# Opening loads of a fused attention and mixture-of-experts kernel: order and queues

## The chip, the cores and the metric

The kernel runs on one core of one Trainium2 chip. The metric is the device time of one execution in microseconds (us); lower is better. The engines are named as the profile names them: PE (TensorE, matrix products; PEld is its weight load), DVE (VectorE), ACT (ScalarE), POOL (GpSimd) and SP (SyncE). SP and ACT can both issue DMAs, each on a queue of its own.

## The reference

The input x has 4 x 1024 tokens of width 256, all in 32-bit floats. Two sandwiches are applied, each adding a normalized result to its input:

```
x = x + layernorm(attention_block(layernorm(x)))
x = x + layernorm(moe(layernorm(x)))
```

The attention block normalizes its input h with a gain and a bias, projects it to q, k, v (256 x 256 each), and does linear attention with 4 heads of 64: q goes through a softmax over the head's 64 channels, k through a softmax over the 1024 tokens, context = k^T v per head, output = q context. A projection wo with a bias bo and a residual follow, then a gelu layer of width 1024 (w_ff1, w_ff2) and a last projection w_d. The second part is a mixture of 8 experts with low-rank updates, of which each token uses its top 2.

## The kernel before, in words

The 4096 tokens are cut into 8 blocks of 512 (BLK), each held as a tile of 128 partitions x 4 tokens x 256; partition p holds tokens 4p to 4p+3 of the block, so a block's rows are contiguous in a partition. The attention part runs block by block through `prelude`, `front` and `middle`; the experts follow on tokens sorted by their pair of experts.

The order of work on PE, DVE, ACT and POOL is fixed when the program is built: the code is written as streams (generators), and a planner with a cost for each step picks the next stream by estimated times (`plan`, `V`, `A`, `G`, and a table `ARRIVE` of assumed arrival times of the first loads). Within an engine instructions run in this order. The first matmuls, the warm-ups of L1886 and L1887 (128 x 128 ones by ones, WARM of them), are issued without adding to the planner's clock. DMAs run in the order in which the program issues them on their queue; the order of the opening ones is written out by hand in L196 to L222.

What the opening consists of, by name and line:

- `load_z(i)` (L170) loads block i's residual x into a tile z. For blocks 0 and 1 it issues two halves, tokens 0 and 1 of each partition on SP's queue and tokens 2 and 3 on ACT's (L180, L181). Later blocks are one DMA on SP's queue.
- `load_w(eng, ...)` (L183) makes a weight tile and loads it on the queue of the engine given.
- `vec` (L197): ten kilobytes of gains and biases. `gate_s` (L201): the router's weights, 8 KB.
- `wq_raw` (L200): the raw query weights, 256 KB, columns 0 to 255 of a 512-column array. `wk_s`, `wv_s`, `wo_s` (256 KB each) and `bo_s` (128 KB as a broadcast) follow on ACT's queue, `wff2_s` (1 MB), `wd_s`, `bd_s`, blocks 2 and 3, `wff1_s` and the experts' weights on SP's.
- `prelude(i)` (L670): on DVE, mean and variance of each of the block's four token columns (`stats`, L340 and L341, a BATCH_NORM_STATS2 and an aggregate each), then `rsqrt2` (L386 on DVE, a power on POOL at L389, result `rr`), then `less_mean` (L395, `lm`) and `normalize` (L404 on DVE, L410 on ACT, alternating for block 0), which writes z in place.
- `prepare_q` (L450): scales the gate by the norm's weights (L454), forms the query bias on PE from wq_raw (`pbq`, L459), scales wq_raw into `wq_s` (first half on ACT, L462; second on DVE, L464), centres the gate (`pcg`, L441, L467), copies it beside wq_s (L469) and the bias into `bq_s` (L473), and scales `wk_s` in place on ACT (L476, L478).
- `front(i)` (L699): transposes z on PE (`pt_h`, L328) and copies it to `hT` on ACT (L719), multiplies by wq_s (`pq`, L734; L315 is the helper that issues matmuls), adds the bias on DVE (L735), then the softmax of q, the keys (`pk`, L769) and so on.

In program order on DVE, block 0's statistics and `r2a` come first, then the two gate scalings, then wq_s (L464), then lm. On ACT, wq_s (L462) comes ahead of block 0's normalization.

Of the kernel before, what the change touches and what calls it, by code (L numbers as in the profile page):

```python
# [15 lines left out]
P = 128  # L16
D = 256
DC = D // P
# [3 lines left out]
E, R = 8, 16  # L22
# [4 lines left out]
TB = 4  # L27
HT = TB // 2
# [12 lines left out]
HALF = P // 2  # L41
CLASSES = ((0, 2), (0, 3), (1, 2), (1, 3), (0, 1), (2, 3))
SHARE = 80
WARM = 14

CODE = (0.0, 1.0, 3.0, 7.0)
KINDS = [CODE[a] + CODE[b] for a, b in (*CLASSES, (0, 0), (2, 2), (1, 1), (3, 3))]
# [19 lines left out]
def sandwich_kernel(  # L67
# [23 lines left out]
    nc = tc.nc  # L91
# [67 lines left out]
    for c in range(DC):  # L159
        t = wp.tile([P, P], F32, tag=f"cbd{c}", name=f"cbd{c}")  # L160
# [4 lines left out]
    xts, zs = {}, {}  # L165

    def tokens(ap, i):
        return ap[i * BLK : (i + 1) * BLK, :].rearrange("(p t) d -> p t d", t=TB)

    def load_z(i):  # L170
        if i in (2, 3):
            zs[i] = sp.tile([P, TB, RW], F32, tag="row", name=f"z_{i}")[:, :, 0:D]
        elif i == NBLK - 1:
            zs[i] = mp2.tile([P, TB, D], F32, tag="u0", name=f"z_{i}")
        else:
            zs[i] = zp.tile([P, TB, D], F32, tag="z", name=f"z_{i}")
        if i > 1:
            nc.sync.dma_start(out=zs[i], in_=tokens(x, i))
            return
        for t, eng in ((0, nc.sync), (HT, nc.scalar)):  # L180
            eng.dma_start(out=zs[i][:, t : t + HT, :], in_=tokens(x, i)[:, t : t + HT, :])  # L181

    def load_w(eng, src, shape, name, pattern=None, **kw):  # L183
        t = wp.tile(shape, F32, tag=name, name=name)
        eng.dma_start(out=t, in_=src.rearrange(pattern, **kw) if pattern else src)
        return t

    def load_ranks(src, name):
# [5 lines left out]
        return t  # L194

    load_z(0)  # L196
    vec = load_w(nc.sync, vecs, [P, 20], "vec")  # L197
    wqv_c = wqv.rearrange("(c p) f -> p c f", p=P)
    wq_raw = mp2.tile([P, DC, D], F32, tag="m1", name="wq_raw")
    nc.sync.dma_start(out=wq_raw, in_=wqv_c[:, :, 0:D])  # L200
    gate_s = load_w(nc.scalar, gate, [P, DC, E], "gate_s", "(c p) f -> p c f", p=P)  # L201
    wk_s = load_w(nc.scalar, wk, [P, DC, D], "wk_s", "(c p) f -> p c f", p=P)
    load_z(1)
    wv_s = wp.tile([P, DC, D], F32, tag="wv_s", name="wv_s")
    nc.scalar.dma_start(out=wv_s, in_=wqv_c[:, :, D : 2 * D])
    wo_s = load_w(nc.scalar, wo, [P, DC, D], "wo_s", "(c p) f -> p c f", p=P)
    bo_s = load_w(nc.scalar, bo.partition_broadcast(P), [P, D], "bo_s")
    wff2_s = mp1.tile([P, FC, D], F32, tag="actA", name="wff2_s")
    nc.sync.dma_start(out=wff2_s, in_=wff2.rearrange("(c p) f -> p c f", p=P))
    wd_s = wp.tile([P, DC, DX], F32, tag="wd_s", name="wd_s")  # L210
# [1 line left out]
    bd_s = wp.tile([P, DX], F32, tag="bd_s", name="bd_s")  # L212
    nc.sync.dma_start(out=bd_s[:, 0:D], in_=bd.partition_broadcast(P))
    load_z(2)
    load_z(3)
    wff1_s = load_w(nc.sync, wff1, [P, DC, FF], "wff1_s", "(c p) f -> p c f", p=P)
# [75 lines left out]
    def psum(name):  # L292
        last[0] = slots.index(min(slots))
        slots[last[0]] = 1e9
        pool, tag = homes[last[0]]
        return pool.tile([P, BLK], F32, tag=tag, name=name)
# [1587 lines left out]
    with tc.manual_schedule(engines={EN.PE, EN.DVE, EN.Activation, EN.Pool}):  # L1884
        warm = psum("warm")
        for _ in range(WARM):  # L1886
            nc.tensor.matmul(warm[:, 0:P], lhsT=ones, rhs=ones, start=True, stop=True)  # L1887
# [154 lines left out]
```

## Time and profile before

| | us |
|---|---|
| median of 3 runs (979.72 to 980.01) | 980.0 |
| profiled execution | 980.27 |
| span of the profiled execution, first to last instruction | 978.2 |
| PE busy | 960.9 |
| first warm-up matmul starts, last one ends | 1.13, 6.12 |
| first matmul on loaded data (pbq) | 8.38 |
| first query projection (pq) | 10.99 |
| last matmul ends | 968.6 |

The mean granted clock of TensorE is 0.998 of full speed. [...] An idle engine costs time only if the work that ends last hangs on it. DMA rows on SPq and ACTq show the issuing alone; the data land later, which is seen in the rows that wait for them.

The opening issues, from the timeline (start on its queue in us): on SP block 0's first half 0.74, vec 1.18, wq_raw 1.65, block 1's first half 2.12, wff2 4.14, wd 8.85, bd 9.28, block 2 9.80, block 3 behind it, wff1 11.68, w1 14.69; on ACT block 0's second half 0.74, gate 1.18, wk 1.66, block 1's second half 2.18, wv 4.32, wo 4.73, bo 5.25 (until 6.16).

### The profile page before, as it was taken

The page shows a single profiled execution, that of the slowest core. Times are in us where ns is not written, and L with a number is a line of the kernel's source. Part 1 is how long each engine was busy: PE and PEld are TensorE (multiplying, and loading weights), DVE is VectorE, ACT ScalarE, POOL GpSimd, SP SyncE. Part 2 cuts the span into 40 slices and gives each one's busy share as a digit, 9 for nine tenths or more (in the row PEclk, how much of TensorE's full clock was granted, in tenths as well). Part 3 has the DMA queues.
Part 4 walks back from the last instruction along what each step waited for, and adds up shares of the span by engine and source line. Part 5 has one row for each costly group of instructions (what it writes and reads, how often), then busy time and mean ns, then how long its engine had stood idle before and what let it go on. Part 6 is the DMA issues. An engine that isn't in the chain of part 4 may idle for free. (4 is left out here: it accounts for less than half of the span.)

```text
span 978.2 us, 12098 instructions
## 1 busy us (share of the span) xinstructions
PE 960.9 (98%) x4235; PEld 644.5 (66%) x4235; DVE 466.6 (48%) x1423; ACT 337.9 (35%) x703; POOL 423.2 (43%) x472
## 2 busy tenths in 40 slices
PE   8999999999999999999999999999999999999996
PEld 7778888888888888887664463644636446364444
DVE  7777666656655465556413323333233332323134
ACT  5545644245223113221214425254252542522110
POOL 2101202201321221324745938759387593885442
PEclk9999999999999999999999999999999999999999
DMA  9604610100120111321100201102011020110000
GB/s 298 183 22 130 144 55 12 67 0 17 61 77 12 45 55 23 116 71 40 45 22 1 70 23 44 44 5 69 20 44 43 1 65 3 44 33 22 0 1 24
DMA packets 33745, 50.14 MB, mean 51 GB/s; under 512 B 5296, under 2 KB 24848, under 8 KB 33680
## 3 DMA queue, kind: packets, MB, share of 16 engines
q1 hardware_dynamic: 29088, 39.36, 14.3%
q0 software_dynamic: 3072, 8.51, 2.4%
q10 hardware_dynamic: 1520, 1.45, 0.4%
q8 instruction: 35, 0.57, 0.2%
q14 instruction: 30, 0.25, 0.1%
HBM read 28.18 MB, written 17.19 MB: 46 GB/s over the span
## 5 line engine op out<-in xcount | busy, mean ns | idle before, releaser
L315 PE MATMUL ph<-tT,w_s 128*128 128x512 f32 (+1 forms) x576 | 235.6, 554 | 0.2
L315 PEld LDWEIGHTS ph<-tT,w_s 128*128 128x128 f32 x576 | 105.4, 190 | 122.1 <-issue 110.5
L315 PE MATMUL py<-wff2d,g 128*128 128x264 f32 x512 | 119.2, 386 | 0.0
L315 PEld LDWEIGHTS py<-wff2d,g 128*128 128x128 f32 x512 | 97.3, 190 | 16.6
L1435 DVE TENSOR_TENSOR act<-act,ph 128x512 f32<-128x512 f32 (+1 forms) x96 | 55.8, 594 | 96.5 <-PE ph L315 51.8
L1485 POOL TENSOR_TENSOR actA<-act,act 128x512 f32<-128x512 f32 x32 | 40.6, 1270 | 133.7 <-DVE act L1435 125.5
L1797 ACT COPY py<-ph 128x512 f32<-128x512 f32 x94 | 53.2, 571 | 120.6 <-PE ph L315 119.8
L1426 ACT ACTIVATE act<-ph 128x512 f32<-128x512 f32 (+1 forms) x96 | 48.6, 521 | 117.0 <-PE ph L315 92.5
L315 PE MATMUL pf<-h2T,wff_s 128*128 128x256 f32 x384 | 87.0, 380 | 0.0
L1435 DVE TENSOR_TENSOR act<-act,py 128x512 f32<-128x512 f32 x48 | 32.9, 685 | 103.7 <-ACT act L1426 103.7
L315 PEld LDWEIGHTS pf<-h2T,wff_s 128*128 128x128 f32 x384 | 72.1, 190 | 10.8 <-issue 1.3
L1021 ACT ACTIVATE g<-pf,bff 128x256 f32<-128x256 f32 x128 | 52.1, 475 | 75.5 <-PE pf L315 74.5
L315 PE MATMUL po<-w_s,actA 128*128 128x256 f32 x256 | 60.5, 383 | 0.0
L1245 POOL DMA_INDIRECT rows<-x,to x32 | 33.5, 1047 | 61.8 <-DVE x L1148 18.5
L315 PE MATMUL po<-w_s,actB 128*128 128x256 f32 x256 | 59.3, 379 | 0.0
L315 PEld LDWEIGHTS po<-w_s,actB 128*128 128x128 f32 x256 | 48.6, 190 | 12.2 <-issue 6.2
L315 PEld LDWEIGHTS po<-w_s,actA 128*128 128x128 f32 x256 | 46.9, 190 | 12.4 <-issue 7.0
L315 PE MATMUL ph<-u,bw 32*128 32x512 f32 x192 | 54.4, 640 | 0.0
L315 PE MATMUL py<-u,bw 32*128 32x512 f32 x192 | 54.4, 640 | 0.0
L356 POOL TENSOR_TENSOR rs_x<-rsa_x,neghalf 128x4 f32<-128x4 f32 x15 | 16.1, 1075 | 77.9 <-DVE rsa_x L352 46.1
L1048 DVE TENSOR_TENSOR y<-py,bd_s 128x264 f32<-128x264 f32 x32 | 13.8, 432 | 74.0 <-PE py L315 73.8
L1485 POOL TENSOR_TENSOR actB<-act,act 128x512 f32<-128x512 f32 x31 | 39.7, 1279 | 19.9 <-DVE act L1435 19.9
(300 smaller groups left out, 1605.6 us busy)
## 6 DMA issues: line engine op xcount, KB each, us to landing
rows<-none SPq DMA_DIRECT2D x4, 1052.0 KB
kept<-x SPq DMA_DIRECT2D x8, 526.0 KB
x<-in_x_dram SPq DMA_DIRECT2D x8, 512.0 KB
row<-rows SPq DMA_DIRECT2D x7, 526.0 KB
z<-in_x_dram SPq DMA_DIRECT2D x6, 512.0 KB
w_s<-in_w_dram SPq DMA_DIRECT2D x3, 1024.0 KB
bw<-b_s SPq DMA_DIRECT2D x24, 128.0 KB
wff_s<-in_wff_dram SPq DMA_DIRECT2D x2, 1024.0 KB
```

The costliest lines, as they stand in the source:

```text
L315: nc.tensor.matmul(out_, lhsT=lhsT, rhs=rhs, start=start, stop=stop, **kw)
L356: nc.gpsimd.tensor_tensor(r, a, neghalf[:, 0:n], ALU.pow)
L1021: nc.scalar.activation(g[:, k * W : (k + 1) * W], pf[:, k * W : (k + 1) * W], AF.Gelu_apprx_tanh, bias=bff1_s[:, f : f + 1],)
L1048: nc.vector.tensor_tensor(y[:, j % HT, :], py[:, 0:DX], bd_s, ALU.add)
L1245: ins = nc.gpsimd.indirect_dma_start(out=dst[:, :], out_offset=bass.IndirectOffsetOnAxis(ap=at, axis=0), in_=src, in_offset=None, bounds_c ...
L1426: nc.scalar.activation(to, h, AF.Silu)
L1435: nc.vector.tensor_tensor(to, to, h3, ALU.mult)
L1485: lambda x0=x0, x1=x1, op=op: nc.gpsimd.tensor_tensor(ac, x0, x1, op))
L1797: nc.scalar.copy(py[a], ph[a])
```

## The change

Block 0 is loaded in four quarters, one token column of every partition each, columns 0 and 2 on SP's queue, 1 and 3 on ACT's. Block 1 becomes one DMA on SP's queue. vec and gate move behind the quarters on ACT's queue; wq_raw comes behind the quarters on SP's; block 1, wk, wv, wo and bo follow it on SP's. Three of the fourteen warm-ups go. The whole diff:

```
-WARM = 14
+WARM = 11
...
-        if i > 1:
+        if i:
             nc.sync.dma_start(out=zs[i], in_=tokens(x, i))
             return
-        for t, eng in ((0, nc.sync), (HT, nc.scalar)):
-            eng.dma_start(out=zs[i][:, t : t + HT, :], in_=tokens(x, i)[:, t : t + HT, :])
+        for t in range(TB):
+            eng = nc.scalar if t % 2 else nc.sync
+            eng.dma_start(out=zs[i][:, t, :], in_=tokens(x, i)[:, t, :])
...
     load_z(0)
-    vec = load_w(nc.sync, vecs, [P, 20], "vec")
+    vec = load_w(nc.scalar, vecs, [P, 20], "vec")
+    gate_s = load_w(nc.scalar, gate, [P, DC, E], "gate_s", "(c p) f -> p c f", p=P)
     wqv_c = wqv.rearrange("(c p) f -> p c f", p=P)
     wq_raw = mp2.tile([P, DC, D], F32, tag="m1", name="wq_raw")
     nc.sync.dma_start(out=wq_raw, in_=wqv_c[:, :, 0:D])
-    gate_s = load_w(nc.scalar, gate, [P, DC, E], "gate_s", "(c p) f -> p c f", p=P)
-    wk_s = load_w(nc.scalar, wk, [P, DC, D], "wk_s", "(c p) f -> p c f", p=P)
     load_z(1)
+    wk_s = load_w(nc.sync, wk, [P, DC, D], "wk_s", "(c p) f -> p c f", p=P)
     wv_s = wp.tile([P, DC, D], F32, tag="wv_s", name="wv_s")
-    nc.scalar.dma_start(out=wv_s, in_=wqv_c[:, :, D : 2 * D])
-    wo_s = load_w(nc.scalar, wo, [P, DC, D], "wo_s", "(c p) f -> p c f", p=P)
-    bo_s = load_w(nc.scalar, bo.partition_broadcast(P), [P, D], "bo_s")
+    nc.sync.dma_start(out=wv_s, in_=wqv_c[:, :, D : 2 * D])
+    wo_s = load_w(nc.sync, wo, [P, DC, D], "wo_s", "(c p) f -> p c f", p=P)
+    bo_s = load_w(nc.sync, bo.partition_broadcast(P), [P, D], "bo_s")
```

The planner's costs and its `ARRIVE` table are not touched.

## The prediction

> **What bounds the kernel now.** I read the page first, then the busy time by stretches, and with these the waits and the timeline of the first 20 us. The page and the stretches (columns: from:to, length, then busy time and instructions of PE, PE's weight load, DVE, ACT, POOL, then clock, DMA share, GB/s):
>
> ```profile
> PE 960.9 (98%) x4235; PEld 644.5 (66%) x4235; DVE 466.6 (48%) x1423; ACT 337.9 (35%) x703; POOL 423.2 (43%) x472
> ```
>
> ```profile
> 1.13:4.25 3.12, 3.12 (x14) 3.12 (x15) 0.10 (x1) 0.00 (x0) 2.95 (x59) 1.00 0.71 208
> 4.25:6.12 1.87, 1.87 (x16) 1.69 (x14) 1.77 (x7) 0.00 (x0) 0.15 (x2) 1.00 0.84 272
> 6.12:8.38 2.26, 0.01 (x2) 0.03 (x1) 0.81 (x6) 1.40 (x2) 1.05 (x1) 1.00 0.97 308
> 8.38:10.99 2.61, 2.37 (x17) 2.03 (x17) 2.05 (x12) 2.08 (x5) 0.00 (x0) 1.00 1.08 367
> 10.99:20.00 9.01, 9.01 (x42) 6.40 (x43) 8.60 (x26) 5.99 (x12) 2.50 (x6) 1.00 1.08 372
> 20.00:60.00 40.00, 39.88 (x217) 31.41 (x216) 27.32 (x74) 23.39 (x51) 3.46 (x5) 1.00 0.52 153
> ```
>
> From 10.99 us, when the first query projection (pq) starts, TensorE hardly stops: it idles 0.12 us from 20 to 60, 0.54 from 60 to 440, 2.05 from 440 to 480 and 1.34 from 480 to its last matmul at 968.6. So this change can move the end only by moving that 10.99 us, and whatever it moves there should arrive almost whole at the end. The opening, by the timeline (start, length, engine, line, operation; in brackets the idle time before and what ended it):
>
> ```profile
> 4.15 0.43 DVE L340 BATCH_NORM_STATS2 st_in<-z 128x6 f32<-128x256 f32 x1 [4.15 <-DMA z<-in_x_dram]
> ...
> 6.41 0.17 DVE L386 TENSOR_SCALAR r2a_x<-mv_in 128x4 f32<-128x4 f32 x1
> ...
> 6.67 1.05 POOL L389 TENSOR_TENSOR rr_x<-r2a_x,neghalf 128x4 f32<-128x4 f32 x1 [2.26 <-DVE r2a_x L386]
> 8.27 0.35 DVE L464 TENSOR_SCALAR wq_s<-wq_raw,vec 128x256 f32<-128x256 f32 x1 [1.38 <-DMA wq_raw<-in_wqv_dram]
> ...
> 8.53 0.15 DVE L395 SCALAR_TENSOR_TENSOR lm_z<-mv_in,rr_x 128x4 f32<-128x4 f32 x1
> ...
> 8.72 1.09 ACT L410 ACTIVATE z<-z,lm_z,rr_x 128x256 f32<-128x256 f32 x2
> ...
> 10.35 1.07 ACT L719 COPY hT<-pt_h 128x512 f32<-128x512 f32 x2 [0.53 <-PE pt_h L328]
> ```
>
> Two arrivals set it. Block 0's first half is visible at 4.15; four pairs of statistics, 0.53 us each, lead to r2a at 6.41 and the root on POOL from 6.67 to 7.72. The second is wq_raw: DVE would need it after its gate work, about 6.89, but it comes at 8.27, and the small lm (8.53), which every normalization needs, is queued behind it on DVE although the root was ready at 7.72. From lm the chain runs through the normalized quarters (the last on ACT until 9.81), transposes, the hT copy at 10.35 and pq at 10.99: 2.46 us.
>
> The rate at which data arrives, in forty slices of 0.25 us from 0 to 10 us:
>
> ```profile
> GB/s 0 0 0 0 0 0 0 139 229 377 344 377 377 245 174 131 197 229 246 291 275 254 291 287 303 344 381 311 340 279 262 274 295 299 365 377 393 381 381 373
> ```
>
> Adding slices (rate times 0.25 us): 131 KB have moved at 2.35, 262 KB at 2.72, block 0's 524 KB at 3.50. DVE sees its half at 4.15, so 0.65 us lie between the last bytes in the mean and the release.
>
> **The change, part by part.**
>
> *Block 0 in quarters on two queues (L180).* Two issues become four, two on each queue, 0.39 to 0.47 us each by the rows, so at 0.74 and about 1.18. Statistics of the first quarter can start when it has landed, provided a reader waits only for its own part of the tile. That parts are tracked is seen in the trace: pq's first matmul starts at 10.99 while the two hT copies, 10.35 to 11.42, still run. If SP's quarter arrived alone it would be visible at 2.35+0.65=3.0; if the two queues share evenly, at 2.72+0.65=3.37. An upper bound is today's 4.15. I take 3.3, near the even share, since both queues issue at 0.74. The fourth quarter is needed only at 3.3+3x0.53=4.9 and all of block 0 was in by about 4.15. Then r2a is at 3.3+2.26=5.56, the root starts 0.26 later as today and ends at 5.82+1.05=6.87, lm starts at 6.95 (0.08 from a root to its next user, as POOL's 14.35 to 14.43). Against 8.53: 1.58 us.
>
> *wq_raw right behind it (L200), without vec before it and wk and half of block 1 beside it.* Ahead of its last byte are 524+262 KB, and vec and gate (18 KB) beside it: 804 KB, which today have moved at 4.88, hence visible at 5.5. That estimate was too good before: wq_raw, wk and all ahead of them were 1,066 KB, moved at 5.83, so it should have been visible at 6.5 and came at 8.27, 1.8 later. Bounds 5.5 and 7.3. I take 6, nearer the first, since now only 18 KB ride on the other queue. What does it have to meet? DVE's scaling (0.35) must end by lm at 6.95, ACT's (0.51) by 7.1, and on PE pbq and pcg (1.30 from 8.38 to 9.68) must not delay the last quarter's transpose: all three say about 6.6. So 6 costs nothing; each us past 6.6 costs one.
>
> *vec and gate on ACT's queue.* Third and fourth issues there, about 1.6 to 2.5; needed at r2a+0.09=5.65. Everything issued up to 2.6 and moved by 4.25 (648 KB) is visible near 4.9. Nothing to pay. ACT's queue is then done at 2.5 instead of 6.16, and its table load (6.19 to 7.47) moves ahead; it had 0.79 us to spare and would otherwise bind at 7.47.
>
> *Block 1 whole, and wk, wv, wo, bo on SP.* ACT's queue falls from seven issues to four (two quarters, vec, gate); SP loses vec and has one more piece of block 0 and wk, wv, wo, bo ahead of wff2. SP's waits show what an issue waits for:
>
> ```profile
> SPq L211 <- DMA wk_s<-in_wk_dram: 4.3, 1, 4.3
> ...
> SPq L209 <- DMA z<-in_x_dram: 1.5, 1, 1.5
> ```
>
> wff2, the ninth load or so in order, waited for the first half of block 0, wd for wk: eight are in flight. Now the first eight are four quarters, vec, gate, wq, block 1; wk waits for the first quarter (3.3), then one issue per 0.45 us follows. Block 1 is wanted by DVE at 10.76-1.65=9.1; 804+524=1,328 KB had moved at 6.63, visible 7.3, or 9.1 with the same 1.8 us of lateness. wk is wanted by ACT at 11.31-1.65=9.7 and by pk at 13; 1,590 KB, 7.45+0.65=8.1. wff2 is wanted at 18, block 2 at 17.4; the bytes ahead of them are those of today and the queue starts sooner. The later issues of SP (b1, w3, b3, w2, b2 until 37.5, then x, block 4) go out no later, and the first use of x is L376 at 63.9. If the cover of 1.8 us for block 1 is gone, DVE, 8.6 of 9.0 us busy there, is late by the difference.
>
> *Three fewer warm-ups (L1886).* They add nothing to the planner's clock, so the order of all else stays. Fourteen are 28 records: 14 in the 3.12 us to 4.25 (223 ns each), 14 in the next 1.87 (134 ns). Six fewer at 134 ns end at 5.32 instead of 6.12. PE then waits for wq anyway: nothing, unless the array is slow at pbq. The trace bounds that: the step is 1.07 us ahead of 5.32, and 2.26 us of idling at 6.12 did not undo it (pbq at 379 ns like later ones).
>
> [...]
>
> **The sum.** lm 1.58 earlier. The transposes gain 0.07 more: the last quarter is ready at 9.81 today, but PE, still behind pbq and pcg, transposes it at about 9.68+3x0.13=10.07, 0.26 later, of which a handover (0.05) and a weight load (0.14) remain when PE is free. So pq starts 1.65 us earlier, at 9.34. The profiled execution took 980.27 (span 978.2, 2.1 around it): 978.6. The median, 980.0, is 0.27 below it; against it, 978.4.
>
> **Rivals.**
> 1. *wq_raw still comes last*, at 7.3 by the lateness of before. For it: DVE, ACT and PE all waited for it. Against: its company on the other queue is gone. Gain 8.27-7.3=1.0: 979.0.
> 2. *More than forecast*: the first quarter alone at 3.0 or before, and block 1 or the weights so early that some of the 4 us of later PE idling go too. 1.95 or more: 977.9. Against: both queues issue at once.
> 3. *Absorbed or not split*: DVE waits for the whole tile at 4.15, so lm waits for today's root (7.72, then 7.8): gain 0.7; or DVE, 95% busy up to 20 us, gives it back. 979.3 to 980. Against: the tracked parts above; the same DVE work starts earlier too.
> 4. *Slower*: PE cools. wq_raw is no earlier than today, PE idles from 5.32 for over 3.1 us (as long as it took to speed up) and pbq, the transposes and pq run slow for 3.12 us: 14 records at 89 ns more, 1.25 us, and the wait beyond 8.27 itself, 0.15 us. 981.4. It decides from wq_raw at 8.4 on; past 9.0 it is over 0.2%.
>
> **How the numbers follow.** Forecast 0.57 (978.1 to 978.8), rival 1 0.16, rival 2 0.14, rival 3 0.08, rival 4 0.05. The range 977.7 to 979.4 holds the forecast, most of rivals 1 and 2, 0.82 in all. 0.2%, about what a measurement of this kernel can tell from no change, is 1.96 us, just above the forecast's gain: faster by more 0.20 (rival 2 and the forecast's best end), slower by more 0.04, within 0.76.
>
> **What would show it.** First statistics at 3.3, their four in 0.53 us steps without a wait, r2a at 5.6, root at 5.8, lm at 7.0, pq at 9.3, warm-ups ending at 5.3, no DVE wait for wq_raw that holds lm, no wait for block 1, wk or wff2; PE idle after pq still 4 us. Wrong if statistics start after 3.6, if lm follows wq_raw rather than the root, or if PE shows new gaps between 10 and 60 us.

## The result, and the profile after

| | before | after |
|---|---|---|
| median (range), runs | 979.53 (979.26 to 981.25), 22 | 981.23 (979.74 to 984.86), 22 |
| profiled execution, its span | 980.27, 978.2 | 979.83, 977.8 |
| first statistics (DVE) | 4.15 | 3.86 |
| gate seen by DVE | not waited for | 7.59 |
| wq_raw seen | 8.27 (DVE) | 5.64 (ACT) |
| lm | 8.53 | 8.13 |
| first query projection pq | 10.99 | 10.47 |

The ratio of after to before is 1.0018, with a 95% interval of 1.0011 to 1.0024: the change costs 0.18%, where the forecast was a gain. The profiled execution of after is one of its shortest, and that of before one of its longer ones. A reader who compares only these two sees a gain of 0.44 us.

The page of after, its busy line:

```profile
PE 962.1 (98%) x4229; PEld 644.8 (66%) x4229; DVE 466.8 (48%) x1423; ACT 338.1 (35%) x703; POOL 423.7 (43%) x472
```

PE has six records fewer and is busy 1.2 us longer. The busy time by stretches says where (from:to, length, busy time and instructions of PE, its weight load, DVE, ACT, POOL, then clock, DMA share, GB/s):

```profile
1.13:6.20 5.07, 5.06 (x22) 4.77 (x22) 2.17 (x9) 0.56 (x1) 3.12 (x60) 1.00 0.78 253
6.20:8.76 2.56, 2.06 (x9) 1.54 (x9) 1.25 (x7) 1.67 (x3) 1.05 (x1) 1.00 0.99 331
```

All 22 records of the eleven warm-ups take 230 ns each, so they end at 6.20 and not at the forecast 5.3, and pbq still runs partly slow (1.50 us instead of 1.10). In before the step to 134 ns came after 14 of 28 records. The timeline of after in the opening:

```profile
3.86 0.43 DVE L341 BATCH_NORM_STATS2 st_in<-z 128x6 f32<-128x256 f32 x1 [3.86 <-DMA z<-in_x_dram]
...
5.64 1.28 ACT L463 ACT_TABLE_LOAD   x1 [5.64 <-DMA wq_raw<-in_wqv_dram]
...
6.12 0.17 DVE L387 TENSOR_SCALAR r2a_x<-mv_in 128x4 f32<-128x4 f32 x1
6.37 1.05 POOL L390 TENSOR_TENSOR rr_x<-r2a_x,neghalf 128x4 f32<-128x4 f32 x1 [1.96 <-DVE r2a_x L387]
...
7.59 0.36 DVE L455 TENSOR_SCALAR gate_s<-gate_s,vec 128x8 f32<-128x8 f32 x2 [1.31 <-DMA gate_s<-in_gate_dram]
...
8.13 0.15 DVE L396 SCALAR_TENSOR_TENSOR lm_z<-mv_in,rr_x 128x4 f32<-128x4 f32 x1
...
10.47 0.49 PE L316 MATMUL pq<-wq_s,hT 128*128 128x264 f32 x1 [0.24 <-ACT hT L720]
```

Three things are to be seen. wq_raw comes early, as forecast. The root is ready at 7.42, but lm stands behind the gate's scaling on DVE, and the gate, 8 KB, is seen only at 7.59. And ACT's table load has not moved ahead: it now stands behind the arrival of wq_raw (5.64), where in before it stood behind nothing but ACT's own issues (from 6.19, the last issue ending at 6.16). The rate at which data arrives, in slices of 0.25 us from 0:

```profile
GB/s 1 0 0 0 0 0 0 33 184 180 242 311 381 353 238 270 324 306 287 306 346 314 412 352 329 378 345 329 336 356 365 377 352 258 246 209 213 168 168 156
```

Added up, 262 KB have moved at 3.07 us, against 2.72 in before's profile. The rows of block 0 are 1 KB long now instead of 2 KB, but that this is the reason is not shown: the four profiles with the loads of before reach 262 KB anywhere from 2.72 to 3.03 us (b_w11 the latest), those with quarters from 2.79 to 3.07.

### The profile page after: what moved, and what is told of

It reads as the page before. It is cut to its first block, busy times and chain, and to the rows that moved or that the text cites. A ratio compares the mean times of both kernels' runs of the same rounds, so it can differ in the third digit from the quotient of the medians.

```text
span 977.8 us, 12085 instructions
## 1 busy us (share of the span) xinstructions
PE 962.1 (98%) x4229; PEld 644.8 (66%) x4229; DVE 466.8 (48%) x1423; ACT 338.1 (35%) x703; POOL 423.7 (43%) x472
```

## Three facts about the spans

**What moves pq moves the end.** In most profiles of this study without a fall of the clock after pq, the span is the start of pq plus 967.2 us:

| profile | pq | span | difference |
|---|---|---|---|
| before | 10.99 | 978.2 | 967.2 |
| after | 10.47 | 977.8 | 967.3 |
| b_w18 | 10.15 | 977.3 | 967.2 |
| b_w11 | 10.42 | 977.7 | 967.3 |
| a_w18 | 11.79 | 979.1 | 967.3 |
| a_g11 | 10.21 | 977.4 | 967.2 |
| best_o | 9.43 | 977.0 | 967.6 |

The profiles of a_w14, a_gt14, fill11 and a_again have 967.2 to 967.3 too. Three more full-clock profiles do not: a_g14 (967.6), best14 (967.8) and a_z14 (970.0). In best_o, best14 and a_g14 PE shows a new wait of 0.3 to 0.5 us behind pq that before does not have (best_o's is shown below); a_z14 waits for block 1. So an earlier pq arrives whole at the end unless the new opening also brings a new wait behind it.

**The profile of before was not an ordinary execution.** Its wq_raw came at 8.27 and held lm. With four more warm-ups and the loads of before (b_w18, 979.45 against 979.48 for before beside it) lm waits for the root, not for wq_raw, and so it does in b_w11:

```profile
6.85 0.34 DVE L464 TENSOR_SCALAR wq_s<-wq_raw,vec 128x256 f32<-128x256 f32 x1
7.80 0.17 DVE L395 SCALAR_TENSOR_TENSOR lm_z<-mv_in,rr_x 128x4 f32<-128x4 f32 x1 [0.61 <-POOL rr_x L389]
```

The late wq_raw is no freak either. The fourth profile with these loads, b_w1, has it again:

```profile
7.95 0.35 DVE L464 TENSOR_SCALAR wq_s<-wq_raw,vec 128x256 f32<-128x256 f32 x1 [1.04 <-DMA wq_raw<-in_wqv_dram]
```

So two of four executions wait for it, and one profile can't say which kind is common. The median can: by pq + 967.2 and 2 us around the span, before's median of 979.5 fits pq at 10.2 to 10.3, not 10.99.

**The mean clock of an execution tells a slow window.** In the rows below the clock has two values, 1 and 0.5, and its slow stretches ahead of the end last 3.41 us, a window from here on, or a multiple of it. In best18, in slices of 1 us, it is 0.70 at 453, 0.50 at 454 and 455 and 0.59 at 456, together 3.42 us at half speed. An execution at full speed from the first step on shows 0.996 to 0.998, since the clock falls at the very end (0.78 in the mean over before's last 9.6 us, where PE has no work). One window at half speed takes off another 0.5 x 3.41/978 = 0.0017. So a run at 0.995 or less has at least one slow window behind the first step. The count is a floor: a run at 0.996 can have one too, and a late first step does not show in it at all (b_w1 below). Of 133 runs of before, 10 are at 0.995 or less; of the changed kernel 26 of 34 (16 of 22, 8 of 10 in a repeat, and the profiled executions look1 and look2).

## The experiments

My first theory after the result was that eleven warm-ups no longer carry TensorE to its step; with fourteen on the new loads it wanted about 979.0, and a_w14 gave 980.77. What I tested from there on were two causes, the late gate and a clock that is lost in TensorE's pauses. Rivals: one of the two alone; a fall of the clock much later, in the routing stage; a late table load as the whole cause. "Low clock" counts runs at 0.995 or less. The three last columns are from the profile of each, which is one execution and need not be a common one.

| kernel | median (range), runs | ratio to before, 95% | low clock | gate or wq_raw seen last by DVE | lm | pq |
|---|---|---|---|---|---|---|
| a_w14 | 980.77 (980.07 to 984.15), 12 | 1.0017 (1.0009 to 1.0026) | 3 | gate 8.16 | 8.70 | 11.04 |
| a_w18 | 980.75 (979.62 to 984.18), 11 | 1.0014 (1.0006 to 1.0023) | 2 | gate 8.91 | 9.45 | 11.79 |
| b_w11 | 980.79 (979.29 to 984.6), 11 | 1.0016 (1.0005 to 1.0027) | 3 | no wait | 8.07 | 10.42 |
| b_w18 | 979.45 (979.27 to 981.25), 11 | 0.9999 (0.9990 to 1.0008) | 0 | no wait | 7.80 | 10.15 |
| a_again | 981.37 (980.2 to 982.62), 10 | 1.0020 (1.0011 to 1.0030) | 8 | gate 8.18 | 8.71 | 11.05 |
| a_g14 | 979.84 (979.16 to 981.21), 11 | 0.9999 (0.9990 to 1.0008) | 2 | no wait | 7.07 | 10.19 |
| a_gt14 | 981.2 (979.77 to 983.65), 11 | 1.0018 (1.0009 to 1.0027) | 3 | wq_raw 7.18 | 7.46 | 11.16 |
| a_z14 | 982.33 (982.15 to 983.54), 6 | 1.0031 (1.0019 to 1.0043) | 1 | gate 6.97 | 7.50 | 10.35 |
| a_g11 | 980.63 (979.44 to 982.15), 11 | 1.0010 (1.0001 to 1.0019) | 5 | no wait | 7.36 | 10.21 |
| fill11 | 980.65 (979.93 to 983.36), 11 | 1.0011 (1.0002 to 1.0020) | 2 | gate 7.64 | 8.18 | 10.52 |
| b_w1 | 981.36 (980.16 to 984.06), 10 | 1.0018 (1.0007 to 1.0029) | 0 | wq_raw 7.95 | 8.22 | 12.38 |
| b_gap | 989.86 (988.62 to 990.63), 4 | 1.0096 (1.0078 to 1.0114) | 4 | wq_raw 15.5 | | 19.89 |
| best14 | 979.76 (979.12 to 981.25), 12 | 0.9997 (0.9988 to 1.0006) | 0 | wq_raw 7.64 | 7.91 | 10.36 |
| best18 | 979.9 (978.93 to 981.87), 12 | 0.9997 (0.9988 to 1.0005) | 1 | wq_raw 7.44 | 7.71 | 10.23 |
| b_q | 980.14 (979.71 to 983.0), 11 | 1.0005 (0.9996 to 1.0015) | 2 | wq_raw 6.64 | 7.06 | 11.15 |
| best_o | 978.94 (978.65 to 980.79), 11 | 0.9994 (0.9985 to 1.0003) | 2 | gate 6.55 | 7.09 | 9.43 |

### The loads alone, the warm-ups alone

The change with 14 or 18 warm-ups, and the kernel before with 11 or 18:

```
-WARM = 11
+WARM = 14        # a_w14; 18 in a_w18 and b_w18, and 11 in b_w11, on the loads of before
```

> The changed kernel with fourteen warm-ups again; the new loads stay. Theory A (TensorE is slow for longer in many executions, because eleven warm-ups no longer carry it to its step to full speed): the scatter of the changed kernel (979.7 to 984.9) shrinks to that of before (about 1 us), the granted clock is 0.997 or more in nearly every run, and the median falls to about 979.0, since the profile of the changed kernel has pq 0.5 us earlier. Rival B (the new order of loads makes the runs differ): median still 981 and scatter of 5 us. In both pq stays near 10.5 in the profile.

> The kernel before with eleven warm-ups; its loads are untouched. Theory A: PE then stands idle from about 5.3 to 5.9 until wq_raw at 8.3, so the step to full speed is missed in as many runs as with the change or more: median 981 to 984, scatter of several us, clock down to 0.99. Rival B (loads): 979.5 as before, scatter about 1 us.

> The changed kernel with eighteen warm-ups. In the profile of the changed kernel all eleven warm-ups ran slow, 0.43 us each, so eighteen last to 1.1 + 18x0.43 = 8.8 if the step is late and to about 6.7 if it comes at 4.4. Theory A: no run with a clock under 0.997; median 979 to 979.5 (some runs pay up to 0.5 us because pbq waits for the warm-ups), scatter under 1 us. Rival B: as the changed kernel, 981 with 5 us of scatter.

> The kernel before with eighteen warm-ups, loads untouched. Theory A2 (a window of about 3.4 us in which TensorE is nearly idle halves its clock for at least one window, at some 1.7 us each; the gap of 2.3 us between the last warm-up and wq_raw gives such windows now and then): no run with a clock under 0.996, median 979.5 as before or 0.2 below, nothing over 980.5. Rival G (the low clocks of single runs have nothing to do with the opening): as many low runs as before, about one in nine.

Each half of the change costs by itself: the loads 1.0017, the warm-ups 1.0016. Together they are 1.0018 to 1.0020, so they do not simply add, as far as the intervals let one say. With the change's loads the gate comes late in every profile (7.6 to 8.9), here in a_w14:

```profile
5.66 0.17 DVE L387 TENSOR_SCALAR r2a_x<-mv_in 128x4 f32<-128x4 f32 x1
8.16 0.36 DVE L455 TENSOR_SCALAR gate_s<-gate_s,vec 128x8 f32<-128x8 f32 x2 [2.33 <-DMA gate_s<-in_gate_dram]
8.44 0.35 DVE L465 TENSOR_SCALAR wq_s<-wq_raw,vec 128x256 f32<-128x256 f32 x1
8.70 0.15 DVE L396 SCALAR_TENSOR_TENSOR lm_z<-mv_in,rr_x 128x4 f32<-128x4 f32 x1
```

r2a is 0.75 us earlier than in before and then DVE stands 2.33 us for 8 KB. With 14 or more warm-ups only 5 of 23 runs have a low clock, so what the loads cost there is mainly this wait. More warm-ups on the loads of before (b_w18) change no time: fourteen were enough for those.

### Gate and vec on the other queue

```
-    vec = load_w(nc.scalar, vecs, ...)
-    gate_s = load_w(nc.scalar, gate, ...)
+    vec = load_w(nc.sync, vecs, ...)       # ahead of wq_raw on SP's queue; 14 warm-ups
+    gate_s = load_w(nc.sync, gate, ...)
```

> Fourteen warm-ups, and vec and gate on the SP queue between block 0's quarters and wq_raw, instead of on the ACT queue. [...] Rival D (8 KB in 32-byte rows are slow wherever they stand): gate still after 7, and wq_raw behind it later too; no gain.

```profile
5.83 0.38 DVE L455 TENSOR_SCALAR gate_s<-gate_s,vec 128x8 f32<-128x8 f32 x2
...
7.07 0.17 DVE L396 SCALAR_TENSOR_TENSOR lm_z<-mv_in,rr_x 128x4 f32<-128x4 f32 x1 [0.42 <-POOL rr_x L390]
```

The wait is gone and lm waits for the root, as forecast, 0.12 us later than the forecast's 6.95. The time goes from 980.77 to 979.84, and 8 of the 11 runs are shorter than the shortest of a_w14, so the loss of the loads was the two small loads on ACT's queue. Both moved in this run; of the two the gate was the later one wherever both are seen (in after PE sees vec at 6.46, DVE the gate at 7.59). It does not become a gain; in this profile ACT is late:

```profile
6.35 1.28 ACT L463 ACT_TABLE_LOAD   x1 [6.35 <-DMA wq_raw<-in_wqv_dram]
7.64 0.51 ACT L463 ACTIVATE wq_s<-wq_raw,vec 128x256 f32<-128x256 f32 x1
8.06 1.08 ACT L411 ACTIVATE z<-z,lm_z,rr_x 128x256 f32<-128x256 f32 x2
```

lm is there at 7.2, ACT's two quarters start at 8.06. The order of ACT's built program shows why. In before the first activation carries a single wait (0.79 us, for wq_raw) and the table load ahead of it, 6.19 to 7.47, none. After the change ACT has two loads to wait for, vec's and wq_raw's, and the wait for wq_raw stands ahead of the table load, so that its 1.28 us follow the arrival of wq_raw, seen at 6.35 here and at 5.64 in after. I first tried to pull the table load ahead with a tiny copy on ACT, but that copy came to stand behind wq_raw as well, so this run proves nothing about the table (a_gt14, 981.2). Why it is 1.4 us slower than a_g14, whose loads it shares, is open; in its one profile wq_raw is seen 0.9 us later (7.18 against 6.30) and pq starts at 11.16:

```
+    touch = sm.tile([P, 1], F32, tag="touch", name="touch")
+    nc.scalar.copy(touch, neghalf[:, 0:1])
```

> As the last kernel (fourteen warm-ups, vec and gate on SP's queue ahead of wq_raw), with one tiny ACT copy of a constant column put right behind ACT's DMA issues, so that ACT's table load no longer stands behind the wait for wq_raw. Theory E (the change moved the table load behind the arrival of wq_raw, where it costs up to 1.3 us): the load is done before 4 us, ACT's scaling of wq_raw starts when wq_raw lands (6.3), ACT's first normalization at 7.3 instead of 8.06, pq at 9.4 instead of 10.2, and the runs with a clock of 0.996 or more have a median of 978.9 instead of 979.6. Rival F (something further on is the bound from 10 us on, DVE for one, so the start gains nothing): pq at 9.4 and still 979.6.

### What makes the gate late

Block 1, with rows of 4 KB, moved behind the weights (14 warm-ups, gate on ACT's queue as in the change):

```
     nc.sync.dma_start(out=wq_raw, ...)
-    load_z(1)
     wk_s = ...
...
     bo_s = ...
+    load_z(1)
```

> The changed kernel with fourteen warm-ups, vec and gate on ACT's queue as in the change, and block 1's load put behind wk, wv, wo and bo, so that rows of 1 KB and not of 4 KB run beside the small rows. [...] Rival H (the small rows are late for any company on the other queue): gate at 7.5 or later.

The gate is seen at 6.97 instead of 8.16, ahead of the 7.5 or later of rival H, and earlier than in any of the seven profiles with block 1 beside it (7.59 to 8.91). So block 1 on SP's queue holds it back on ACT's, by 0.6 to 1.9 us from this one profile to those seven, though not alone: the gate still comes last of all that DVE needs. Whether it is block 1's rows of 4 KB or its 512 KB the run does not separate. The kernel loses on another side, where the prediction had put block 1's cover:

```profile
6.97 0.36 DVE L455 TENSOR_SCALAR gate_s<-gate_s,vec 128x8 f32<-128x8 f32 x2 [0.98 <-DMA gate_s<-in_gate_dram]
...
12.88 0.43 DVE L341 BATCH_NORM_STATS2 st_in<-z 128x6 f32<-128x256 f32 x1 [3.55 <-DMA z<-in_x_dram]
```

DVE stands 3.55 us for block 1, and PE waits for it later, 1.0 us at pbdt (behind hT) and 0.5 at pt_h: 982.33. These are 1.5 of the 2.8 us by which its span exceeds pq + 967.2; the rest is not accounted for.

Another queue is not enough to make the gate late. In b_q (below) it is on ACT's queue as well, but issued one place earlier, with block 1 still in halves, and DVE uses it almost at once, 0.1 to 0.2 us behind r2a (one profile):

```profile
5.93 0.37 DVE L459 TENSOR_SCALAR gate_s<-gate_s,vec 128x8 f32<-128x8 f32 x2
```

The rows say where the gate was late (7.59 to 8.91 with block 1 whole on the other queue, 6.97 without it) and where it was not (no wait in a_g14, on SP's own queue ahead of wq_raw). No run here shows single packets, so by what the other queue delays it stays open.

### What TensorE's pauses cost

Bounds first: the kernel before with one warm-up, and with wq_raw behind wff2, wd and bd, so that PE idles for long.

> The kernel before with a single warm-up. Theory A2: TensorE is at half speed in pbq, the transposes and pq, until a window of about 3.4 us is busy, which pq's start at about 10.5 to 11 allows at 14 to 17.5; the matmuls in between take twice as long, so that 3.4 to 6.8 us of slow work cost 1.7 to 3.4 us: 981.2 to 983 in every run, and in the profile pq's matmuls stand 0.48 us apart and not 0.24. Rival G: 979.5, since the opening waits for data anyway.

> The kernel before with fourteen warm-ups, wq_raw's load moved behind wff2, wd and bd on its queue, which makes a gap of some 6 us in TensorE's work after it was warm. It measures a fall of the clock by itself: theory A2 wants the matmuls after the gap to be slow again for one or two windows, and the span to be pq's start plus 967.2 plus 1.7 or 3.4; rival G wants pq's start plus 967.2 with matmuls at full speed.

With one warm-up the step comes at 13.7 us, pq at 12.38, and the cost is 1.8 us. (The clock column shows 1.00 ahead of an execution's first step, though the matmuls are slow there, pbq 2.05 us instead of 1.10, so this kernel counts no low clock.) In b_gap, PE is idle for 8.64 us, and the clock falls for three windows. The columns are as above:

```profile
2.81:6.22 3.41, 3.41 (x18) 3.41 (x18) 1.74 (x7) 0.00 (x0) 1.44 (x23) 1.00 0.95 264
6.22:9.64 3.42, 0.72 (x6) 0.52 (x5) 0.83 (x5) 0.00 (x0) 1.05 (x1) 1.00 1.06 369
9.64:13.05 3.41, 0.00 (x0) 0.00 (x0) 0.00 (x0) 0.00 (x0) 0.00 (x0) 0.50 1.10 347
13.05:16.46 3.41, 0.88 (x2) 0.82 (x3) 0.99 (x4) 0.95 (x1) 0.00 (x0) 0.50 1.10 350
16.46:19.88 3.42, 3.42 (x15) 2.93 (x14) 1.58 (x11) 2.42 (x5) 0.00 (x0) 0.50 1.03 402
```

In this trace a window with little work is followed by a slow one, and the full window at the end by a fast one. The profiles below do not all keep to that.

Then the changed kernel itself, once more timed (a_again), and two single executions of it with a profile each (look1, look2), in the hope of one of its longer ones:

> The changed kernel itself once more, beside the others of this call. Theory A2: two thirds of the runs or more have a clock of 0.995 or less, and they lie near 981.3, 983 and 984.6, one, two and three windows of 1.7 us above 979.7. If the profiled run is one of them, its opening shows matmuls at twice the usual spacing somewhere between 6 and 17 us, after they had been fast. Rival G: the times of low-clock runs are not grouped, and the profile shows slow matmuls elsewhere.

> The changed kernel itself, once more, for a profile of an execution that is one of its longer ones. Sixteen of its 22 runs and 8 of 10 of the repeat show a mean granted clock of 0.995 or less, against 0.996 to 0.998 of the profiles read so far. Theory A (the opening): TensorE is idle between the weight bias product and the gate's correction, and the clock falls, or rises late, in the opening; then the first query product starts at 11 us as before or later, and its matmuls are 0.2 us or more apart; span 979 to 980.5. Theory B (the routing stage): the opening is as in the profiles read so far, and the clock falls for 3.4 us near 453 us, behind TensorE's pause of 0.97 us there. If the execution is again a short one (span below 978.5), nothing follows.

> As the first look: a second execution of the changed kernel, to see where the clock falls if it does. Theory A: in the opening, before 15 us. Theory B: near 453 us.

Both are longer ones. The second took 981.32, close to the median of 981.23 (columns as above; then, from its timeline, PE):

```profile
6.17:9.59 3.42, 1.95 (x11) 1.36 (x10) 1.52 (x9) 2.46 (x4) 1.05 (x1) 1.00 1.05 283
9.59:13.00 3.41, 3.41 (x12) 2.53 (x12) 3.03 (x17) 2.39 (x5) 0.10 (x1) 0.50 0.97 279
13.00:16.41 3.41, 3.41 (x15) 2.69 (x15) 2.61 (x6) 2.17 (x5) 2.03 (x6) 1.00 1.09 351
```

```profile
6.23 1.10 PE L316 MATMUL pbq<-wq_raw,vec 128*128 128x256 f32 x4
8.52 0.58 PE L316 MATMUL pcg<-gate_s,ones 128*128 128x8 f32 x4 [1.19 <-DVE gate_s L455]
9.35 2.04 PE L329 MATMUL pt_h<-ident,z 128*128 128x128 f32 x8 [0.25 <-DVE z L405]
11.21 4.70 PE L316 MATMUL pq<-wq_s,hT 128*128 128x264 f32 x16
```

By its time this is a typical run of the changed kernel. After the warm-ups PE stands 1.19 us for the gate; in the window from 6.17 to 9.59 it is busy 1.95 of 3.42 us; at 9.59 the clock falls to half for one window, and the transposes (2.04 instead of 1.48) and the first query products (4.70 instead of 3.87) are slow. Its gate comes at 8.19 and lm at 8.72, as in a_w14, whose pq starts at 11.04 at full clock. So against b_w18 (pq 10.15, 979.33 for the profiled execution) the new loads with their late gate cost 11.04 - 10.15 = 0.89, the slow window 11.21 - 11.04 = 0.17 ahead of pq and 979.2 - 11.21 - 967.2 = 0.8 behind it: 1.9 in all, and 981.32 - 979.33 = 2.0 was measured.

look1 took 984.24 and lost two windows in the opening and a third in the routing stage:

```profile
9.07:12.48 3.41, 3.27 (x14) 2.37 (x14) 3.27 (x17) 2.53 (x5) 0.00 (x0) 0.50 0.92 301
12.48:15.89 3.41, 3.41 (x9) 2.68 (x9) 1.43 (x7) 1.98 (x5) 2.13 (x6) 0.50 1.09 351
...
456.21:459.62 3.41, 3.41 (x13) 2.30 (x10) 3.31 (x8) 0.66 (x2) 3.24 (x3) 0.50 0.00 0
```

The second slow window follows one in which PE was busy 3.27 of 3.41 us, so a busy window at half clock does not always bring the clock back. In both profiles the changed kernel loses its clock in the opening, and the rival of the routing stage is an addition to it that comes in other kernels too (best18 below).

The pause was then filled with four more matmuls of ones between pbq and pcg:

```
         pw = psum(name)
+        for _ in range(4 if name == "pcg" else 0):
+            nc.tensor.matmul(pw[:, 0:P], lhsT=ones, rhs=ones, start=True, stop=True)
```

> The changed kernel with four more matmuls of ones on ones, put between the weight bias product and the gate's correction, so that TensorE is busy in the wait for the gate. Loads and warm-ups are those of the change. Theory A (the pause in the opening costs the clock): fewer runs at 0.995 or below (under a third of them), and a median near that of the change with 14 warm-ups or below, 980.2 to 980.8. Theory B (routing stage) or theory C (the three warm-ups ahead of everything matter, not the pause): no difference, 981.2 to 981.4 with two thirds of the runs at 0.995 or below. If the gate comes early, the four matmuls delay the query product by up to 0.9 us: then 981 at a clean clock.

Only 2 of 11 runs have a low clock, against 26 of 34 without the four matmuls, on the same loads and warm-ups. So the pause is what costs the changed kernel its clock in most runs. What that is worth in time is less sure: the median falls from 981.23 to 980.65, near that of a_w14, but the intervals overlap. Either remedy, three more warm-ups ahead of the pause (3 of 12 low) or four matmuls in it, keeps the clock in most runs, and neither removes the wait for the gate.

And the gate early again, with eleven warm-ups:

> The changed kernel with the small vectors and the gate on SyncE's queue ahead of the raw query weights, as in the run that did that with 14 warm-ups (979.84), but with the change's 11 warm-ups. If the three warm-ups cost by themselves, whatever the gate does: near 981, half of the runs or more at a clock of 0.995 or below. If they cost only together with the pause for the gate: 979.6 to 980.0, as with 14. If fewer warm-ups were worth something: below 979.5.

980.63 with 5 low clocks of 11, against 979.84 with 2 of 11 for a_g14. In its profile the last warm-up ends at 5.24 and pbq waits 1.19 us for wq_raw. By the medians the three warm-ups cost here too, with no wait for the gate, though the intervals of the two (1.0001 to 1.0019 and 0.9990 to 1.0008) overlap.

### Is there a version that gains?

The table load pulled ahead by hand (the tiny copy first on ACT, in the hand-written order), on the loads of a_g14, with 14 and with 18 warm-ups:

> Fourteen warm-ups, vec and gate on SP's queue ahead of wq_raw, and the tiny ACT copy now placed by hand ahead of all other ACT work, so that the table load really comes first (in the last try it stood behind wq_raw again). In all profiles so far the span is pq's start plus 967.1 to 967.6. Theory E: table load done by 4 us; lm at 7.1 to 7.5 (first quarter visible 3.4 to 3.9, or wq_raw at 7.2), pq 2.46 to 2.6 later, 9.6 to 10.0, span 976.7 to 977.2, best runs near 978.8, median 979.2 or below. Rival F: pq no earlier than 10.2.

> The same with eighteen warm-ups. Theory A2 (idle windows halve the clock): fewer runs far above the lowest than with fourteen; median 979.2 or below, at most one of eleven above 980.5. Against it: if the step to full speed comes late, the warm-ups last until 7 to 8 and hold pbq and the transposes, up to 0.5 us. Rival G: as many high runs as with fourteen.

The table load now runs at 1.66 to 2.94 us, but the time stays with before's, where I had forecast 979.2 or below. In the two profiles wq_raw is seen at 7.64 and 7.44 and holds lm. It stands behind the gate's 256 short rows on SP's queue, but that alone is not the reason: a_g14 and a_g11 have the same order of issues on that queue, wq_raw's starting at 2.59 as here, and see it at 6.30 and by 6.41, a_gt14 at 7.18. So one load arrives up to 1.3 us apart in different executions of the same queue order, and what makes it late is open. The profile of best18 fell into a loss of clock far from the opening, after a pause of 0.97 us at 450:

```profile
450.00:453.41 3.41, 2.44 (x16) 1.79 (x16) 1.56 (x5) 1.46 (x5) 0.00 (x0) 1.00 0.00 0
453.41:456.82 3.41, 3.41 (x13) 2.27 (x12) 3.31 (x9) 0.66 (x2) 3.08 (x3) 0.50 0.00 0
```

Its span is 969.5 us more than its pq, that of best14 967.8. The 1.7 between them agree with half of 3.41, the price of one window in full work.

Then the quarters alone, on all else as before, and the gate behind wq_raw on SP's queue:

```
+    nc.sync.dma_start(out=wq_raw, in_=wqv_c[:, :, 0:D])
     gate_s = load_w(nc.sync, gate, ...)
-    nc.sync.dma_start(out=wq_raw, in_=wqv_c[:, :, 0:D])     # best_o, from best14
```

> The kernel before with one part of the change alone: the first residual in four quarters on the two queues. Everything else, 14 warm-ups, block 1 in halves, the weights on both queues, is as before. If the quarters by themselves are worth something: the statistics start 0.2 to 0.6 us earlier, the root ends near 7.2 to 7.5, and the time is 978.9 to 979.3. If the raw query weights or the function table set the opening's end instead: 979.4 to 979.8, as before. The quarters shift which transfer the last load of ScalarE's queue waits for, ahead of the table; if that wait comes late, ScalarE is late and the time is 980 or more.

> The version with vec and the gate on SyncE's queue, 14 warm-ups and the function table loaded first, with the gate now behind the raw query weights instead of ahead of them. If the small rows of the gate held the raw query weights back: these are seen near 6.5 to 7.0 instead of 7.64, the query product starts near 9.9 to 10.1, and the median is 979.0 to 979.4, below that of the kernel before. If the gate then comes late instead: it is waited for until 7.5 or later, and the time is 980 or more. If neither moves: 979.7 to 979.9.

The quarters alone are worth nothing measurable (980.14). The profile is of one of the longer runs (982.10, with a slow window behind pq), so it tells the order of things and not the price. In it lm comes at 7.06, but ACT's last issues go out later than before (the last one ends at 7.28 instead of 6.16), and the table load stands behind them:

```profile
6.34 0.94 ACTq L190 DMA_DIRECT2D bo_s<-in_bo_dram  x1
7.31 1.28 ACT L467 ACT_TABLE_LOAD   x1 [7.31 <-DMA z<-in_x_dram]
8.61 0.51 ACT L467 ACTIVATE wq_s<-wq_raw,vec 128x256 f32<-128x256 f32 x1
9.02 1.07 ACT L415 ACTIVATE z<-z,lm_z,rr_x 128x256 f32<-128x256 f32 x2
```

best_o is the forecast's opening at last (from its timelines of DVE and of PE):

```profile
3.42 0.43 DVE L341 BATCH_NORM_STATS2 st_in<-z 128x6 f32<-128x256 f32 x1 [3.42 <-DMA z<-in_x_dram]
...
6.55 0.36 DVE L455 TENSOR_SCALAR gate_s<-gate_s,vec 128x8 f32<-128x8 f32 x2 [0.70 <-DMA gate_s<-in_gate_dram]
...
7.09 0.16 DVE L396 SCALAR_TENSOR_TENSOR lm_z<-mv_in,rr_x 128x4 f32<-128x4 f32 x1
```

```profile
6.42 1.10 PE L316 MATMUL pbq<-wq_raw,vec 128*128 128x256 f32 x4 [0.38 <-DMA wq_raw<-in_wqv_dram]
7.35 0.51 PE L316 MATMUL pcg<-gate_s,ones 128*128 128x8 f32 x4
7.72 1.48 PE L329 MATMUL pt_h<-ident,z 128*128 128x128 f32 x8
9.43 3.87 PE L316 MATMUL pq<-wq_s,hT 128*128 128x264 f32 x16 [0.24 <-ACT hT L720]
```

Statistics at 3.42, lm at 7.09, pq at 9.43; 978.94, and 8 of its 11 runs (978.65 to 979.18) are shorter than the shortest of 21 runs of before beside it (979.25). By the interval of the ratio (0.9985 to 1.0003) no gain is proved. Against best14 only the gate's place differs, and wq_raw is seen by 6.42; whether the gate's new place did that or the scatter of its arrival, one profile of each can't tell. Of the 0.8 us that pq is earlier than in an ordinary run of before, 0.4 are lost at a new wait (the waits of PE: line waited for, us in total, times, longest):

```profile
PE pt_q L329 <- DVE bv L493: 0.4, 1, 0.4
```

It is at 22.6 us, where PE reaches the transposes of q ahead of a small copy that stands in DVE's queue. best14 has the same wait (0.5) with pq at 10.36, so it is not the early pq alone that brings it. In these versions DVE is the next bound in the opening, as the busy 8.60 of 9.01 us had let one expect.

## Why the prediction was wrong, step by step

- **Block 0 in quarters** (3.3): right in kind. Quarters are tracked one by one, and the first is seen at 3.40 to 3.86, 0.1 to 0.6 us late, by the execution.
- **wq_raw at 6**: right, 5.6 to 6.8 in the profiles of the changed kernel.
- **vec and gate, "nothing to pay", near 4.9**: the step that failed. I counted the bytes ahead of the gate as if all queues shared one stream in order of issue, and put its wait at nothing. It was seen at 7.59 to 8.91, 2.7 to 4 us later, and lm is queued behind its scaling. With 14 warm-ups, undoing this alone (a_g14) gives back 0.93 us.
- **The table load "moves ahead"**: wrong. ACT's first activation now had a wait for vec and one for wq_raw to keep, and the table load came behind the latter. Covered in the changed kernel, where the gate is later still. In a_g14's profile it keeps ACT from lm for 0.8 us and so takes the gain; the runs that moved it (best14, best18) had wq_raw late in their profiles and do not price it alone.
- **Block 1, wk and the rest covered**: right; statistics of block 1 start at 9.74 in after with no wait. Moved behind the weights the cover is gone (a_z14).
- **Three fewer warm-ups, "nothing"**: the second step that failed. By themselves they cost 1.0016 (b_w11). The two observations I leaned on, a step 1.07 us ahead of the last warm-up and 2.26 us of idling that did not undo it, were one execution: in after the step had not come when the warm-ups ended at 6.20, though before had it at 4.25, and in look2 a pause of 1.19 us was enough to lose it. In b_w11 only 3 of 11 runs have a low clock, so part of its 1.2 us is not accounted for. A late first step, which the clock column does not show, is a candidate that no profile of b_w11 settles.
- **The gain arrives whole**: right, pq + 967.2, to 0.4 us in best_o and 0.6 in best14.
- **The base**: lm at 8.53 was a late arrival of that one execution; where lm waits for the root it is 7.8 to 8.1 (b_w18, b_w11), and the median fits that. So 0.5 to 0.7 of the 1.58 us was no gain to be had, and taking another 0.27 off for the median counted it twice. best_o has nearly the forecast's pq (9.43 against 9.34) and takes 978.94, by another order of loads.

Of the rivals, the fourth had one of the two causes, matmuls that run slow behind a pause, and nearly the time (981.4); that the time fits is luck, since the late gate, which it does not have, makes up about half of the loss (0.89 of 1.9 us in look2). Its condition was wrong too: it wanted PE idle for over 3.1 us for wq_raw, and here a pause of 1.2 us for the gate did it. The clock fell after windows in which PE was busy 1.95 of 3.42 us (look2) and 2.44 of 3.41 (best18). The share of busy time alone does not decide it: the repeat of the changed kernel (a_again) kept its clock after a window with 1.80 of 3.41 (5.18 to 8.59). What does is open.

## What to carry to other kernels

Bytes ahead of a load are no estimate of its arrival, of a small one least of all. Here the gate was in time ahead of wq_raw on the same queue (used at 5.83 with no wait, a_g14), 0.70 us late behind it (6.55, best_o), and 1.3 to 2.9 us late on the other queue beside block 1 (7.59 to 8.91); where a small load stands early in an engine's order, try its place before counting on it. Before a wait is priced from one profile, see in a second execution that it is there at all: wq_raw was seen up to 1.3 us apart with the same order of loads. Time in which TensorE only waits is not free for its warm-ups: a pause behind them, 1.19 us in look2 and 1.26 in a_again, costs a window of half clock in some runs and none in others, so it shows in the median and hardly in one profile.

## What the runs showed of the hardware that I had not expected

- An 8 KB load with short rows took 5.0 us or more from the end of its issue (2.6) to its use (7.59 to 8.91) beside block 1 on the other queue, 4.4 without block 1 (a_z14), and 3.5 when it stood behind wq_raw on the same queue (best_o, from 3.07 to 6.55).
- TensorE's clock falls after some partly idle windows (1.79, 1.95 and 2.44 of 3.4 us busy) and not after another (1.80 in a_again); a slow window cost 1.0 us in look2, where the work in it still waited in part, and 1.7 in best18. With eleven or more warm-ups the first step came anywhere from 4.1 to 7.3 us, a spread of nearly one window of 3.41, though they start at 1.13 or 1.14 in every profile (4.06 in a_g11, 7.25 in after).
- A pause of 0.97 us near 450 us, which the profiles of before and after have too at full clock, is followed by a slow window in some executions (best18, look1).
